# Linear-size squared attention in a hybrid network: look-ahead of the key projections, place of one copy, and place of a yield in the feed-forward

## The chip, the cores and the metric

One Trainium2 chip, one NeuronCore of it. The metric is device time in microseconds from launch to end, all inputs and outputs in HBM, everything in float32. The five engines have queues of their own that run in order: TensorE (PE in the profile, PEld for its weight loads), VectorE (DVE), ScalarE (ACT), GpSimd (POOL) and SyncE (SP), which only issues transfers here. Matmul results go to PSUM, eight banks of 2 KiB per partition.

## The reference

The network has two layers. The first is a 7x7 pairwise self-attention convolution on four images of 256 x 56 x 56; the change doesn't touch it. The second works on the 3136 pixels of each image as tokens of 256 channels: normalise, attend with squared scores, normalise, route half of the tokens through a feed-forward.

```python
qkv = x @ qkv_w.T + qkv_b                      # 8 heads of 32
scores = jnp.einsum('bnhd,bmhd->bhnm', q, k) * scale
t = jnp.square(scores + 5.0)
attn = t / jnp.sum(t, axis=-1, keepdims=True)
out = jnp.einsum('bhnm,bmhd->bnhd', attn, v).reshape(B, N, D)
return out @ proj_w.T + proj_b
...
weights = (jnp.einsum('bsd,do->bso', x, wr) + br)[..., 0]
_, idx = jax.lax.top_k(weights, k)             # k = 1568, of which 1567 are used
h = jax.nn.gelu(jnp.einsum('bkd,dh->bkh', sel, w1) + b1)
y = (jnp.einsum('bkh,hd->bkd', h, w2) + b2) * w_sel[..., None]
processed = jnp.zeros_like(x).at[batch_idx, sel_idx].set(y)
return processed + x
```

## The kernel before

The square of a score is a polynomial of second degree in the key, so no score is ever formed. For each image and each group of four heads a **key stage** runs over 25 tiles of 128 tokens and sums products of key features with the values; the result is a small matrix of coefficients. A **query stage** per image then makes the same features of the queries and multiplies them with the coefficients.

The order of the work is the order in which the program text issues it: each engine keeps that order (`InOrder`), and a tile framework puts semaphores where one instruction needs another or a buffer. Side jobs are generators in a list `later`. `aside()` (line 1678) moves each of them on by one step, and `run(steps)` calls it once after every step of the main work. `run_fast` (line 1844), used in the feed-forward, calls it twice.

A key stage is `keys(b, g)`, line 1198. Three functions make up a tile m:
- `tokens(m)` (line 1203) projects the tokens into keys and values: eight TensorE matmuls into `pv`. One PSUM tile of two banks, `held["kv"]`, takes two tiles of tokens, the even one in the first bank and the odd one in the second; there are two such PSUM tiles (pool `mm`, `bufs=2`). ScalarE copies the keys into `ls` (five buffers) and the values into `v`.
- `features(m)` (line 1223) makes the products of keys with keys, `phi` (two buffers): the squares on ScalarE, eleven of the fifteen remaining distances on VectorE, which reads the keys from PSUM, the others on GpSimd.
- `add(m, phi)` (line 1241) adds values times features into two PSUM banks: `accs` takes the products `phi`; `accq` takes the last distance, the linear sums and, from column P on, the second moments of the keys.

The loop at line 1265 calls `tokens` for the first three tiles, and then at each step `features(m)`, `add(m - 1)`, `tokens(m + 3)` and a `yield`, at which the side jobs run. The first step of image b + 1 is issued inside the query stage of image b.

`coefficients(b, g)`, line 1278, is a side job. Its first step reads `accs` and `accq` in several VectorE instructions and makes `st`; its second makes `line` from column P of `accq`, its third `second` from the next 32 columns (line 1322). `accs` and `accq` lie in a pool of two buffers (`accp`), so the next stage's first `add` needs them free. Further side jobs during a first group (g = 0) are the division, output projection and normalisation of the image before: `divide`, `tokens_out` (po, tk, st, uw in the profile); during a second group the projection of the first queries.

The **feed-forward** takes the 6268 chosen tokens in 13 parts of up to 512. `turn` transposes a part, `first` multiplies by the first weights (ph) with the GELU on ScalarE, `second` (line 1805) by the second weights: for each half of a part 32 matmul instructions (py), then VectorE adds the bias (fz), scales and adds (fy), and GpSimd scatters the rows to the output. While the first parts run, the selection of the last image, `select(b)` (line 1581), is still a side job: eight rounds in which VectorE compares and counts (good, digit, bits, base, tried, hit, per), and TensorE adds the counts over the partitions (pn); then the places (pm, pae, pbe, pas, pbs) and 28 scatters of rows by GpSimd. Parts from number 9 on contain rows of that image; SyncE fetches them after those scatters.

Of the kernel before, what the change touches and what calls it, by code (L numbers as in the profile page):

```python
# [7 lines left out]
F32 = mybir.dt.float32  # L8
I32 = mybir.dt.int32
AF = mybir.ActivationFunctionType  # L10
ALU = mybir.AluOpType
# [4 lines left out]
P = 128  # L16
# [13 lines left out]
DH = 32  # L30
# [6 lines left out]
NT = (HW + P - 1) // P  # L37
# [984 lines left out]
def attn_ffn_layers(  # L1022
# [40 lines left out]
    cp = inner.enter_context(tc.tile_pool(name="coef", bufs=2))  # L1063
    stp = inner.enter_context(tc.tile_pool(name="sums", bufs=1))
    qp = inner.enter_context(tc.tile_pool(name="q", bufs=2))
    ve, te, se, sy, gp = (
        InOrder(tc, e) for e in (nc.vector, nc.tensor, nc.scalar, nc.sync, nc.gpsimd)
    )
# [9 lines left out]
    for i, tag in enumerate(("t", "t", "tr")):  # L1078
        both = tp.tile([P, 2, CH], F32, tag=tag, name=f"rs0_{i}")
        f = slice((2 * i + 1) * CH, (2 * i + 3) * CH)  # L1080
# [10 lines left out]
    kb = const.tile([P, 2, 2 * DH], F32, name="kb")  # L1091
# [102 lines left out]
    def further(a, n):  # L1194

        return bass.AP(a.tensor, a.offset, [*a.ap[:-1], [1, n], a.ap[-1]])

    def keys(b, g):

        vs, ks = {}, {}  # L1200
        size = lambda m: min(P, HW - m * P)

        def tokens(m):

            mn = size(m)
            if m % 2 == 0:
                held["kv"] = mm.tile([P, 2, 512], F32, tag="mm", name=f"pv_{b}_{g}_{m}")
            p = held["kv"][:mn, m % 2]
            for c in range(2):
                matmul(  # L1210
                    p[:, : 2 * P], xn[:, c, m * P : m * P + mn],
                    wqkv[:, c, C:].rearrange("p (i o) -> p i o", i=2)[:, :, g * P : (g + 1) * P],
                    start=c == 0, stop=c == 1,
                )
            k = ks[m] = p[:, :P].rearrange("p (h e) -> p h e", e=DH)
            se.activation(
                lss[m % NKV][:mn, :, LK:LS].rearrange("p h (i e) -> p h i e", i=2),
                k.unsqueeze(2).to_broadcast([mn, 4, 2, DH]), AF.Identity,
            )
            v = vs[m] = kp.tile([P, P], F32, tag="v", name=f"v_{b}_{g}_{m}", bufs=5)  # L1220
            se.activation(v[:mn], p[:, P : 2 * P], AF.Identity)

        def features(m):

            mn = size(m)
            ls, k = lss[m % NKV], ks.pop(m)
            phi = php.tile([P, 4, NF], F32, tag="phi", name=f"phi_{b}_{g}_{m}")
            mine = ls[:mn, :, LK : LK + DH]
            se.activation(phi[:mn, :, :DH], mine, AF.Square)
            at = phi[:mn, :, DH:].rearrange("p h (l e) -> p h l e", e=DH)  # L1230
            for e, of, a, z in ((ve, k, 0, FAR), (gp, mine, FAR, HALF - 1)):
                e.tensor_tensor(
                    at[:, :, a:z], of.unsqueeze(2).to_broadcast([mn, 4, z - a, DH]),
                    further(ls[:mn, :, LK + 1 + a : LK + 1 + a + DH], z - a), ALU.mult,
                )
            gp.tensor_tensor(
                ls[:mn, :, :HALF], mine[:, :, :HALF], mine[:, :, HALF:], ALU.mult
            )
            return phi

        def add(m, phi):
            mn = size(m)
            v, ls = vs.pop(m), lss[m % NKV]
            first, last = m == 0, m == NT - 1
            if first:
                held["sums", b, g] = [
                    accp.tile([P, 512], F32, tag="acc", name=f"acc{i}_{b}_{g}") for i in "sq"
                ]
            accs, accq = held["sums", b, g]
            for h, r in enumerate(QUARTERS):  # L1250
                te.matmul(accs[r], v[:mn, r], phi[:mn, h], start=first, stop=last)
            for h, r in enumerate(QUARTERS):
                te.matmul(
                    accq[r, : LK + DH], v[:mn, r], ls[:mn, h, : LK + DH], start=first, stop=last,
                    skip_group_check=True,
                )

            for h, r in enumerate(QUARTERS):
                k = ls[:mn, h, HALF : LK + DH]
                te.matmul(  # L1260
                    accq[r, P : P + 1 + DH], k[:, 1:], k, start=False, stop=last,
                    skip_group_check=True,
                )

        for m in range(3):
            tokens(m)
        waiting = None
        for m in range(NT):
            phi = features(m)
            if waiting:  # L1270
                add(*waiting)
            waiting = m, phi
            if m + 3 < NT:
                tokens(m + 3)
            yield
        add(*waiting)

    def coefficients(b, g):

        at = f"{b}_{g}"  # L1280
        accs, accq = held.pop(("sums", b, g))
# [2 lines left out]
        ve.tensor_copy(v1, accq[:, HALF:LK])  # L1284
        lin = stp.tile([P, 2 * DH], F32, tag="lin", name=f"lin_{at}")
        linear = accq[:, LK : LK + DH]
        ve.scalar_tensor_tensor(
            lin.rearrange("p (i e) -> p i e", i=2), kb[:, g].rearrange("p (i e) -> p i e", i=2), v1,
            linear.unsqueeze(1).to_broadcast([P, 2, DH]), ALU.mult, ALU.add,
# [15 lines left out]
        ve.tensor_copy(st[:, NF + DH :], lin[:, :DH])  # L1305
        yield

        line = cp.tile([P, 3], F32, tag="line", name=f"line_{at}")
        ve.tensor_copy(line[:, 0:1], accq[:, P : P + 1])
        ve.tensor_scalar(line[:, 1:2], col(f"k_{g}"), float(HW), None, ALU.mult)  # L1310
        ve.tensor_tensor(line[:, 1:2], line[:, 1:2], line[:, 0:1], ALU.add)
        ve.tensor_scalar(line[:, 2:3], line[:, 1:2], 2 * CSHIFT, None, ALU.mult)
# [6 lines left out]
        )  # L1319
        second = stp.tile([P, DH], F32, tag="second", name=f"second_{at}")  # L1320
        ve.scalar_tensor_tensor(
            second, kb[:, g, :DH], line[:, 0:1], accq[:, P + 1 : P + 1 + DH], ALU.mult, ALU.add
        )
        ve.scalar_tensor_tensor(
            second, p[:, :DH], col(f"k_{g}"), second, ALU.mult, ALU.add
        )
        gram = cp.tile([P, P], F32, tag="gram", name=f"gram_{at}")
# [78 lines left out]
    def queries(b):  # L1406
# [54 lines left out]
        if b + 1 < NB:  # L1461
            held["keys"] = keys(b + 1, 0)
            next(held["keys"])
# [286 lines left out]
    for b in range(NB):  # L1750
        held["keys only"] = True
        for g in range(2):
            if g and b + 1 < NB:
                held["t", b + 1, 0] = load(b + 1, 0, "t")
            run(keys(b, g) if b == 0 or g else held.pop("keys"))
            later.append(coefficients(b, g))
            aside()
            if g == 0:
                later.append(project(b, 0))
        later.extend(whole)  # L1760
        whole.clear()
        held["keys only"] = False
        run(queries(b))
# [41 lines left out]
    def second(i):  # L1805

        rows, h = held.pop(("part", i)), held.pop(("h", i))
        y = fp.tile([P, 4, C], F32, tag="y", name=f"fy_{i}")
        for j, (_, pn) in enumerate(parts[i]):

            ve.tensor_scalar(
                y[:pn, j], rows[:pn, j, :C], rows[:pn, j, C + 3 : C + 4],
                rows[:pn, j, C + 2 : C + 3], ALU.mult, ALU.add,
            )
        for m in range(0, len(parts[i]), 2):
            p = accp.tile([P, 2, C], F32, tag="acc", name=f"py_{i}_{m}")
            z = fp.tile([P, 2, C], F32, tag="z", name=f"fz_{i}_{m}")
            both = parts[i][m : m + 2]
            for j, (_, pn) in enumerate(both):
                f = slice((m + j) * P, (m + j) * P + pn)  # L1820
                for e in range(FF // P):
                    te.matmul(
                        p[:pn, j], h[:, e, f], w2[:, e], start=e == 0 and j == 0,
                        stop=e == FF // P - 1, skip_group_check=True,
                    )
            pn, n = both[-1][1], len(both)
            ve.tensor_tensor(
                z[:pn, :n], p[:pn, :n], b2[:pn].to_broadcast([pn, n, C]), ALU.add
            )
            for j, (_, pn) in enumerate(both):  # L1830
                ve.scalar_tensor_tensor(
                    y[:pn, m + j], z[:pn, j], rows[:pn, m + j, C : C + 1], y[:pn, m + j],
                    ALU.mult, ALU.add,
                )
                gp.indirect_dma_start(
                    out.rearrange("b n c -> (b n) c"),
                    bass.IndirectOffsetOnAxis(
                        ap=rows.bitcast(I32)[:pn, m + j, C + 1 : C + 2], axis=0
                    ),
                    y[:pn, m + j], None,  # L1840
                )
            yield

    def run_fast(steps):
        for _ in steps:
# [195 lines left out]
```

## Time and profile before

Three runs took 3243.72, 3245.78 and 3254.06 us, median 3245.78. The profiled execution took 3248.73 us, with a span of 3247.0 us between its first and last instruction and a mean granted TensorE clock of 0.988.

| stretch | us from the span's start |
|---|---|
| convolution layer | 0 to 1442 |
| key stages of image 0, first and second group | 1442 to 1504, 1504 to 1566 |
| query stage of image 0 | 1566 to 1777 |
| key stages of image 1 | 1777 to 1848.5, 1848.5 to 1911 |
| key stages of image 2 | 2133 to 2207.5, 2207.5 to 2270 |
| key stages of image 3 | 2492 to 2565, 2565 to 2628 |
| query stage of image 3 | 2628 to 2845 |
| feed-forward | 2845 to 3247 |

| instruction group | count | mean ns |
|---|---|---|
| TensorE pv, 128x256 | 3136 | 386 |
| VectorE phi, 128x1408 | 200 | 1618 |
| GpSimd phi, 128x512 | 200 | 1241 |
| ScalarE ls, 128x256 | 200 | 387 |

In lines of the profile, `out<-in` names tiles with buffer numbers left out, sizes are partitions x elements, `xN` counts instructions, and a bracket at the end gives idle time of the engine ahead of the line and what ended it. Matmuls overlap, so a TensorE line's duration is longer than its share of the time; distances between starts say more. A line of the timeline begins with start and duration. Nearly all instructions carry one line number, 1007, that of the helper which keeps the order, so groups are told apart by tile names.

### The profile page before, as it was taken

The page shows a single profiled execution, that of the slowest core. Times are in us where ns is not written, and L with a number is a line of the kernel's source. Part 1 is how long each engine was busy: PE and PEld are TensorE (multiplying, and loading weights), DVE is VectorE, ACT ScalarE, POOL GpSimd, SP SyncE. Part 2 cuts the span into 40 slices and gives each one's busy share as a digit, 9 for nine tenths or more (in the row PEclk, how much of TensorE's full clock was granted, in tenths as well). Part 3 has the DMA queues.
Part 4 walks back from the last instruction along what each step waited for, and adds up shares of the span by engine and source line. Part 5 has one row for each costly group of instructions (what it writes and reads, how often), then busy time and mean ns, then how long its engine had stood idle before and what let it go on. Part 6 is the DMA issues. An engine that isn't in the chain of part 4 may idle for free. (4 is left out here: it accounts for less than half of the span.)

```text
span 3247.0 us, 108290 instructions
## 1 busy us (share of the span) xinstructions
PE 3002.4 (92%) x47224; PEld 1311.2 (40%) x47224; DVE 2226.9 (69%) x3019; ACT 1576.1 (49%) x2947; POOL 1726.2 (53%) x1223
## 2 busy tenths in 40 slices
PE   5999999999999999988999799988899899988998
PEld 2333333333333333334333343334333433355666
DVE  4888889898888889888555866568656765443111
ACT  4556556665666665533455344543455345521111
POOL 2898898899989989976200530246022521201311
PEclk9999999999999999999999999999999999998999
DMA  8656676566665756430022102310133001311110
GB/s 233 170 150 176 159 184 183 131 185 179 173 164 155 191 142 163 116 129 19 22 71 57 39 6 65 95 46 20 39 83 82 14 14 48 115 54 35 57 51 23
DMA packets 276497, 327.54 MB, mean 101 GB/s; under 512 B 95985, under 2 KB 269461, under 8 KB 275893
## 3 DMA queue, kind: packets, MB, share of 16 engines
q1 hardware_dynamic: 266037, 298.84, 34.9%
q0 software_dynamic: 7824, 19.48, 1.8%
q8 instruction: 371, 6.08, 0.8%
q10 hardware_dynamic: 2160, 2.29, 0.2%
q14 instruction: 105, 0.86, 0.1%
HBM read 251.51 MB, written 68.51 MB: 99 GB/s over the span
## 5 line engine op out<-in xcount | busy, mean ns | idle before, releaser
L1007 ACT ACTIVATE ph<-pg,unit 128x896 f32<-128x896 f32 x448 | 427.0, 1004 | 402.2 <-PE pg L1007 384.5
L1007 PE MATMUL acc<-pr,same 128*32 128x448 f32 x5376 | 596.7, 545 | 17.9 <-POOL pr L1007 12.0
L1007 POOL TENSOR_TENSOR phi<-ls 128x512 f32<-128x512 f32 (+1 forms) x200 | 248.2, 1241 | 455.7 <-issue 226.3
L1007 POOL TENSOR_TENSOR pr<-xw,w 128x1792 f32<-128x1792 f32 (+2 forms) x126 | 413.6, 3307 | 109.6 <-ACT exp L1007 84.3
L1007 DVE TENSOR_TENSOR pr<-xc,exp 128x1792 f32<-128x1792 f32 (+2 forms) x247 | 441.6, 1839 | 34.4 <-ACT exp L1007 29.9
L1007 DVE TENSOR_TENSOR pr<-xw,exp 128x1792 f32<-128x1792 f32 (+1 forms) x252 | 447.5, 1804 | 2.4 <-DMA xw<-x3d 1.4
L1007 POOL TENSOR_TENSOR pr<-xc,w 128x1792 f32<-128x1792 f32 (+1 forms) x135 | 419.8, 3120 | 12.6 <-ACT w L1007 7.1
L1007 POOL DMA_INDIRECT us<-rows,to x112 | 113.3, 1011 | 576.9 <-DVE rows L1007 334.6
L1007 DVE TENSOR_TENSOR phi<-pv,ls 128x1408 f32<-128x1408 f32 (+1 forms) x200 | 320.8, 1618 | 42.3 <-PE accs L1007 34.5
L1007 PE MATMUL quad<-y,cw 32*32 32x224 f32 (+1 forms) x10752 | 299.3, 456 | 35.1 <-ACT w L1007 19.0
L1007 PE MATMUL pg<-qT,pairs 32*128 32x448 f32 x1792 | 277.2, 588 | 5.7 <-ACT ph L1007 5.3
L1007 PE MATMUL pv<-early,xn 128*32 128x256 f32 x3136 | 213.9, 386 | 58.0 <-DVE phi L1007 40.2
L1007 ACT ACTIVATE ls<-pv 128x256 f32<-128x256 f32 (+1 forms) x200 | 77.4, 387 | 340.0 <-PE pv L1007 317.5
L1007 PEld LDWEIGHTS acc<-pr,same 128*32 128x32 f32 x5376 | 132.6, 109 | 243.4 <-issue 145.8
L1007 PE MATMUL accs<-phi,v 128*32 128x512 f32 (+1 forms) x1600 | 214.8, 599 | 13.7 <-DVE phi L1007 12.3
L1007 PE MATMUL acc<-ph,cf 128*32 128x448 f32 (+1 forms) x1792 | 214.8, 551 | 0.0
L1007 ACT ACTIVATE h<-ph,apar 128x512 f32<-128x512 f32 (+1 forms) x104 | 63.3, 659 | 308.8 <-PE ph L1007 308.8
L1007 ACT ACTIVATE y<-quad,bn2t,bn2s 128x896 f32<-128x896 f32 x112 | 164.5, 1468 | 65.3 <-PE quad L1007 65.3
L1007 DVE TENSOR_REDUCE mm<-quad 128x56 f32<-128x1792 f32 x112 | 172.5, 1540 | 32.3 <-PE quad L1007 31.3
L1007 POOL TENSOR_TENSOR y<-a,ac 128x672 f32<-128x672 f32 x112 | 171.1, 1528 | 36.1 <-DMA ac<-a12d 36.1
L1007 ACT ACTIVATE w<-quad,par 128x1792 f32<-128x1792 f32 x112 | 154.3, 1378 | 69.8 <-PE quad L1007 69.1
L1007 PEld LDWEIGHTS quad<-y,cw 32*32 32x32 f32 x10752 | 85.5, 103 | 249.3 <-issue 119.2
(284 smaller groups left out, 4925.7 us busy)
## 6 DMA issues: line engine op xcount, KB each, us to landing
xw<-x3d SPq DMA_DIRECT2D x54, 992.0 KB
xc<-x3d SPq DMA_DIRECT2D x58, 248.0 KB
xc<-x3d SPq DMA_DIRECT2D x58, 247.5 KB
xc<-x3d SPq DMA_DIRECT2D x58, 247.0 KB
xc<-x3d SPq DMA_DIRECT2D x58, 246.5 KB
x3d<-sx SPq DMA_DIRECT2D x28, 496.0 KB
xr<-in_x_own SPq DMA_DIRECT2D x56, 224.0 KB
xs<-xr SPq DMA_DIRECT2D x224, 56.0 KB
```

What stands on the lines that cost most here:

```text
L1007: return lambda *a, **k: self.tc.keep_in_program_order(of(*a, **k))
```

## The change

There are three edits. The key projections run two tiles ahead of the products instead of three. The second moments (column P and the 32 after it) are copied out of `accq` into a new tile `moments` early in the first step of `coefficients`, and later steps read the copy; `line` is allocated earlier. In `second` the `yield` moves from the end of the loop's body to between the matmuls and VectorE's read of their result, so that the side jobs of that step are issued ahead of fz, fy and the output scatters. There are eight new VectorE instructions in all, one per key stage.

```diff
-        for m in range(3):
+        for m in range(2):
             tokens(m)
         waiting = None
         for m in range(NT):
...
             if waiting:
                 add(*waiting)
             waiting = m, phi
-            if m + 3 < NT:
-                tokens(m + 3)
+            if m + 2 < NT:
+                tokens(m + 2)
             yield
         add(*waiting)
...
         linear = accq[:, LK : LK + DH]
+        line = cp.tile([P, 3], F32, tag="line", name=f"line_{at}")
+        moments = stp.tile([P, 1 + DH], F32, tag="moments", name=f"moments_{at}")
+        ve.tensor_copy(moments, accq[:, P : P + 1 + DH])
...
-        line = cp.tile([P, 3], F32, tag="line", name=f"line_{at}")
-        ve.tensor_copy(line[:, 0:1], accq[:, P : P + 1])
+        ve.tensor_copy(line[:, 0:1], moments[:, 0:1])
...
-            second, kb[:, g, :DH], line[:, 0:1], accq[:, P + 1 : P + 1 + DH], ALU.mult, ALU.add
+            second, kb[:, g, :DH], line[:, 0:1], moments[:, 1:], ALU.mult, ALU.add
...
                         p[:pn, j], h[:, e, f], w2[:, e], start=e == 0 and j == 0,
                         stop=e == FF // P - 1, skip_group_check=True,
                     )
+            yield
             pn, n = both[-1][1], len(both)
             ve.tensor_tensor(
                 z[:pn, :n], p[:pn, :n], b2[:pn].to_broadcast([pn, n, C]), ALU.add
             )
...
                     y[:pn, m + j], None,
                 )
-            yield
```

## The prediction

> **What bounds the kernel now.** I read the page first: TensorE is busy 92% of the span, and the granted clock is full nearly everywhere. The change touches two stretches only: the eight key stages (four images, two groups of heads, 25 tiles each) and the feed-forward at the end. So I went to what TensorE waits for in each.
>
> ```profile
> PE 3002.4 (92%) x47224; PEld 1311.2 (40%) x47224; DVE 2226.9 (69%) x3019; ACT 1576.1 (49%) x2947; POOL 1726.2 (53%) x1223
> ```
>
> The table of TensorE's waits over the stretch with the key stages (1442 to 2628; columns: sum, times, longest):
>
> ```profile
> PE pv L1007 <- DVE phi L1007: 40.2, 37, 3.9
> PE accs L1007 <- DVE phi L1007: 12.3, 29, 0.9
> PE accq L1007 <- DVE second L1007: 9.6, 4, 2.4
> ```
>
> These are the waits the change aims at: a projection (pv) held until VectorE's products (phi) leave the PSUM tile that is reused, and four sums (accq) held by the late read of the second moments. Together 49.8 us, 1.5% of the span. The same stretch in order of time, in a stage with no side work:
>
> ```profile
> 1536.62 1.07 PE L1007 MATMUL pv<-early,xn 128*32 128x256 f32 x16
> 1537.50 1.04 PE L1007 MATMUL accs<-phi,v 128*32 128x512 f32 x8
> 1538.51 1.05 PE L1007 MATMUL pv<-early,xn 128*32 128x256 f32 x16
> 1538.78 1.62 DVE L1007 TENSOR_TENSOR phi<-pv,ls 128x1408 f32<-128x1408 f32 x1 [0.35 <-PE accs L1007]
> 1539.69 0.39 ACT L1007 ACTIVATE ls<-pv 128x256 f32<-128x256 f32 x1 [1.12 <-PE pv L1007]
> 1539.97 0.27 ACT L1007 ACTIVATE v<-pv 128x128 f32<-128x128 f32 x1
> 1540.46 0.85 PE L1007 MATMUL pv<-early,xn 128*32 128x256 f32 x12
> ```
>
> Two tiles take 1540.46 - 1536.62 = 3.84 us, with TensorE idle under 0.1 of it. So in steady state there is almost nothing to win; the waits sit where VectorE has side work. Now the opening of the stage of image 1, where two tiles share one PSUM tile just as everywhere:
>
> ```profile
> 1778.15 0.27 ACT L1007 ACTIVATE v<-pv 128x128 f32<-128x128 f32 x1
> ...
> 1778.47 1.93 PE L1007 MATMUL pv<-early,xn 128*32 128x256 f32 x32 [0.67 <-ACT v L1007]
> ...
> 1779.89 0.27 ACT L1007 ACTIVATE v<-pv 128x128 f32<-128x128 f32 x1
> 1780.25 1.62 DVE L1007 TENSOR_TENSOR phi<-pv,ls 128x1408 f32<-128x1408 f32 x1 [2.40 <-ACT v L1007]
> ```
>
> The products of tile 0 need only tile 0, whose copies ended at 1778.42. They start at 1780.25, when ScalarE has copied tile 1 out of the other half. So the products of an even tile wait for projection and copies of the odd tile beside it: 1780.25 - 1778.47 = 1.78 us after that projection starts. Today that is paid once per stage, because projections run three tiles ahead.
>
> Feed-forward, TensorE alone:
>
> ```profile
> 2900.18 7.07 PE L1007 MATMUL py<-xn,h 128*128 128x256 f32 x32
> 2911.15 0.25 PE L1007 MATMUL pn<-per,aones 112*32 112x15 f32 x8 [3.90 <-DVE per L1007]
> 2911.33 8.86 PE L1007 MATMUL py<-xn,h 128*128 128x256 f32 x32
> 2924.11 0.30 PE L1007 MATMUL pn<-per,aones 112*32 112x15 f32 x8 [3.92 <-DVE per L1007]
> 2924.34 6.12 PE L1007 MATMUL ph<-fu,xn 128*128 128x512 f32 x8
> ```
>
> The counting matmul pn of the last image's selection stands behind a batch of py, and its input (per) stands on VectorE behind fz and fy, which wait for that batch. TensorE idles 3.9 us, and the next batch runs slowly: 8.86 for what took 7.07. The windows name the cause; the third number from the end is the granted clock:
>
> ```profile
> 2900.00:2907.30 7.30, 7.25 (x36) 6.07 (x33) 2.53 (x6) 1.91 (x4) 0.00 (x0) 1.00 0.00 0
> 2911.30:2920.20 8.90, 8.89 (x40) 7.18 (x33) 0.00 (x0) 0.00 (x0) 0.96 (x1) 0.81 0.22 66
> 2924.30:2930.40 6.10, 6.10 (x18) 2.39 (x11) 2.02 (x7) 0.00 (x0) 0.96 (x1) 0.59 0.35 99
> ```
>
> Granted clock 1.00 before the wait, 0.81 and 0.59 after.
>
> **Keys two ahead.** No instruction is added. Projection of tile m+2 now follows the sums of tile m-1. It reuses a tile read by products m-1 at the latest, which those sums needed anyway: the 40.2 us wait goes. In exchange the odd neighbour m+1 is projected just before the sums of m-1, and the even products m wait for its copies. With S the start of the even sums: next projection S + 1.01 (1537.50 to 1538.51), neighbour copied and products start 1.78 later, the sums that wait for them start 1.77 after that (1560.22 to 1561.99 in this trace). Pair: 1.01 + 1.78 + 1.77 = 4.56 against 3.84, +0.72. TensorE's own work is 2 x (1.01 + 0.87) = 3.76, so it idles 0.8 per pair. What is queued behind the late products on VectorE is the odd tile's products, 1.53 later and in time, and the side jobs; behind the waiting sums on TensorE is the next projection.
>
> I then walked each kind of stage tile by tile: an instruction starts when its engine is done with the one ahead and what it waits for has ended, with these spacings and with the side jobs at the durations of their rows. The walk of the old order gives 62.2, 71.1 and 58.5 us, the trace 62.5 (1503.90 to 1566.4), 71.7 (1776.76 to 1848.5) and 61.9 (1442.0 to 1503.9).
> - Second group, four stages: the sums of tile 6 come 3.8 us earlier (24.2 into the stage, not 28.0), since the 2.39 us hold of accq and the pv waits in the coefficients' side work are gone. From there to tile 22 seven pairs lose 0.72 each and the eighth, which had no projection ahead of its sums, 1.5: 6.6. The last tiles return 0.4: 64.7 against 62.2, +2.4 each, +9.6.
> - First group of images 1 to 3: side work of VectorE (statistics 1.6, uw 1.9, scaling 2.0, waits for po) reaches to tile 16. There the old projections waited 9.9 to 11.2 us; tile 16 comes 4.1 earlier (51.5, not 55.6), three clean pairs lose 2.6, the end returns 0.4: 69.2 against 71.1, -1.9 each, -5.7.
> - First stage: one scaling of 1.0 each third tile, which falls into VectorE's new slack; ten pairs lose 0.7 each: +6 (walk +6.6).
> Sum +10. The price of a pair is what the trace of before cannot show in steady state. 51 pairs carry it (32, 9 and 10); at half of 0.72 the sum is 18 lower, at one and a half times 18 higher: bounds -8 and +28. I take the full 0.72, since each of its three parts is a row.
>
> The wait for the neighbour is one place to weigh a rule. The Trainium skill, PSUM — Partial Sum Buffer, section on bank collisions, asks for guards by bank and quadrant. Tile 0 and tile 1 lie in different banks, so by it the products need not wait for the neighbour; the row above (2.40 us) shows that here they do. What the bank rule would make of the time is the first rival.
>
> **Moments copied first.** Eight copies of 128x33 from PSUM, not in the trace: between 0.14 (copy of 128x1) and 0.28 (lin, 128x64), taken as 0.19. Four lie ahead of the first products of a second group (in the walk), four at the start of the queries, where VectorE idles 1.42 before them; uncovered they cost 0.8 in all. Alone the edit frees little: the projection behind accq waited for the same products, ended 1513.83, and ran at 1514.27. It pays only together with the shorter look-ahead.
>
> **Feed-forward.** No instruction is added; TensorE's order stays. On VectorE the selection's chain (good to per, 2908.81 to 2911.01, 2.2 us) moves ahead of fz and fy, so it runs under the 7.07 us of py. Removed: 3.90 + 3.92 + 3.92 (2950) + 2.96 (pm, 2964) = 14.7. After a second half, fz and fy come between: py end to pn is then 3.9, and a ph batch of 3.70 plus 0.18 covers it; nothing new. With the waits goes the slow running: 8.86 - 7.07, 6.12 - 3.70, 10.03 - 7.07, 5.10 - 3.70 = 8.6. Sum -23.3, bounds -13 and -24. On POOL two row scatters now go ahead of two output scatters (2.85 us apart, so 5.7 later); the rows of part 9, which SP fetches behind them until 3105, are used at 3140.7. SP's order stays. The tail from 3000 on is TensorE without gaps, so the gain reaches the end.
>
> The second place: the Trainium skill, TensorE: Matmul & The Clock Gate, Part 1, says half rate follows an idle window of about 3.4 us and lasts about as long. By it three waits are long enough and cost 1.7 each, an estimate of 5.1 instead of 8.6 and 3236 for the sum; the rows also show 5.10 for 3.70 after a wait of 2.96, so the rows stand.
>
> **Sum.** 3248.73 (profiled execution, span 3247.0) + 10 - 23.3 = 3235.4. It lay 3.0 above the median of the runs, 3245.78, so 3232 there.
>
> **Rivals.**
> 1. The products wait by bank only. Then no pair is slower: the same walk gives 57.9, 64.9 and 56.4, so 4 x -4.3, 3 x -6.2, -2.1 = -38; with -23.3: 3185. For it: no data of the neighbour is used. Against it: the 2.40 us row.
> 2. Slower: the neighbour's copies set the pace in all stages, with no early gains, because side work sits in VectorE's program order between even and odd products and delays both. 12 pairs x 0.72 x 8 = +69, less 23.3: +46, 3291; it decides from where the stages lose over 2.9 us each (23.3 / 8). For it: VectorE is busy 56 of 73 us in image 1. Against it: its waits on the sums, up to 0.7 a tile, shrink with the old pv wait.
> 3. No change: the clock also stays low behind the 1.8 us wait for per_sign (2891.8), which is not touched, and only the waits go: +10 - 14.7, 3241.
>
> **Chances.** Forecast 0.68 (own range 3219 to 3243), rival 1 0.06, rival 2 0.14, rival 3 0.12. 0.3% is 9.7 us, about what a measurement can tell from none. Faster: 0.56 of the forecast plus rival 1, 0.62; same: 0.12 + 0.12 + 0.01, 0.25; slower 0.13. Range: -8 - 24 gives 3214, +28 - 13 gives 3261, of which I leave out the top, where both bounds would have to meet: 3214 to 3257.
>
> **What would show it.** Right: products of even tiles waiting for ACT v in all stages, pairs of 4.5 to 4.6 us, no accq wait for second, pv waits gone; no pn wait over 0.5 after 2890 and py at 7.07. Wrong: pairs of 3.8 (rival 1), or first-group stages longer than 74 us (rival 2), or a granted clock under 0.9 after 2900 (rival 3).

## The result, and the profile after

The changed kernel takes 3223.69 us (median of six, 3218.65 to 3233.17), the kernel before 3245.38 (six, 3243.39 to 3254.06). The ratio is 0.993, 95% interval 0.9908 to 0.9951: faster by 16 to 30 us. The forecast was 3232, in a range of 3214 to 3257.

The profiled execution of the changed kernel is the longest of its six, 3233.17 us with a span of 3231.4. Cut at the same marks as the kernel before (a key stage ends with the copy of `v1` out of accq, which the trace prints as v<-accq; the feed-forward starts with the first ft), the two spans compare as follows:

| stretch, us | before | changed | difference |
|---|---|---|---|
| convolution, to the first pv | 1442.0 | 1451.1 | +9.1 |
| first stage, image 0 | 62.1 | 69.1 | +7.0 |
| first groups of images 1, 2, 3 | 71.9, 74.8, 73.7 | 69.2, 69.3, 69.9 | -2.6, -5.6, -3.9 |
| second groups of images 0 to 3 | 62.4, 62.7, 62.4, 62.4 | 64.5, 64.5, 64.5, 63.7 | +2.1, +1.8, +2.1, +1.3 |
| query stages, sum | 870.3 | 871.0 | +0.7 |
| feed-forward, to the end | 402.3 | 374.7 | -27.6 |

The key stages together lose 2.3 us. The feed-forward makes the whole gain. The convolution, whose code is the same, varies: it ended between 1432.1 and 1451.1 us in the nine profiled executions of this study. Its +9.1 here lies within that range. This execution lies 9.5 above its kernel's median; how much of that is the convolution can't be said, since each kernel has one trace.

The page of the changed kernel:

```profile
PE 2998.0 (93%) x47224; PEld 1309.7 (41%) x47224; DVE 2217.6 (69%) x3027; ACT 1574.0 (49%) x2947; POOL 1724.8 (53%) x1223
```

VectorE has eight instructions more (3027 against 3019), the copies of the moments; nothing else is new. TensorE's waits over the key stages (sum, times, longest):

```profile
PE accs L1007 <- DVE phi L1007: 28.1, 42, 7.8
PE accs L1007 <- POOL phi L1007: 18.1, 32, 0.8
PE accs L1007 <- ACT v L1007: 15.8, 26, 0.6
```

No projection waits for products any more (40.2 us before), and accq no longer waits for second (9.6). In their place the sums accs wait, 62 us in these three rows where 12.3 stood. Together TensorE's waits inside the eight stages come to 84.8 us, against 80.4 before: they moved and did not leave. What VectorE waits for tells why, first before and then changed:

```profile
DVE phi L1007 <- ACT v L1007: 7.5, 4, 2.4
DVE phi L1007 <- ACT v L1007: 85.9, 63, 3.2
```

Before, it came four times, all in the first groups of images 1 to 3, and not once in every stage as the prediction says. Now it comes 63 times, in all eight stages, for 96 even tiles that have an odd neighbour (12 in each stage). One steady pair in order of time:

```profile
1555.98 0.38 PE L1007 MATMUL pv<-early,xn 128*32 128x256 f32 x1
...
1558.65 0.38 PE L1007 MATMUL pv<-early,xn 128*32 128x256 f32 x1
...
1560.07 0.27 ACT L1007 ACTIVATE v<-pv 128x128 f32<-128x128 f32 x1
...
1560.42 3.15 DVE L1007 TENSOR_TENSOR phi<-pv,ls 128x1408 f32<-128x1408 f32 x2 [1.39 <-ACT v L1007]
...
1560.53 0.38 PE L1007 MATMUL pv<-early,xn 128*32 128x256 f32 x1
```

The projection of the odd neighbour starts at 1558.65, ScalarE has copied it at 1560.34, and only then VectorE makes both tiles' products. The pair takes 1560.53 - 1555.98 = 4.55 us. The feed-forward, TensorE alone:

```profile
2905.60 0.23 PE L1007 MATMUL pnsign<-per_sign,aones 112*32 112x1 f32 x8 [1.81 <-DVE per_sign L1007]
2905.76 3.70 PE L1007 MATMUL ph<-fu,xn 128*128 128x512 f32 x8
...
2910.50 7.07 PE L1007 MATMUL py<-xn,h 128*128 128x256 f32 x32
2917.50 0.25 PE L1007 MATMUL pn<-per,aones 112*32 112x15 f32 x8
2917.68 7.17 PE L1007 MATMUL py<-xn,h 128*128 128x256 f32 x32
```

No bracket at pn, and the second py of the part takes 7.17 us where it took 8.86. From 2849.8 to 3225.3 us the granted clock is 1.00 throughout. The first two lines hold something that the forecast left as it was: behind the wait for per_sign, which is as long as before, ph takes 3.70 us and not 5.40. In the kernel before:

```profile
2893.58 0.23 PE L1007 MATMUL pnsign<-per_sign,aones 112*32 112x1 f32 x8 [1.82 <-DVE per_sign L1007]
2893.75 5.40 PE L1007 MATMUL ph<-fu,xn 128*128 128x512 f32 x8
```

### The profile page after: what moved, and what is told of

It is laid out like the page before. It is cut to its first block, busy times and chain, and to the rows that moved or that the text cites. A ratio compares the mean times of both kernels' runs of the same rounds, so it can differ in the third digit from the quotient of the medians.

```text
span 3231.4 us, 108046 instructions
## 1 busy us (share of the span) xinstructions
PE 2998.0 (93%) x47224; PEld 1309.7 (41%) x47224; DVE 2217.6 (69%) x3027; ACT 1574.0 (49%) x2947; POOL 1724.8 (53%) x1223
## 5 line engine op out<-in xcount | busy, mean ns | idle before, releaser
L1007 DVE TENSOR_TENSOR phi<-pv,ls 128x1408 f32<-128x1408 f32 (+1 forms) x200 | 317.3, 1616 | 87.7 <-ACT v L1007 85.9
L1007 PE MATMUL accs<-phi,v 128*32 128x512 f32 (+1 forms) x1600 | 214.5, 602 | 74.9 <-DVE phi L1007 28.1
L1007 ACT ACTIVATE y<-quad,bn2t,bn2s 128x896 f32<-128x896 f32 x112 | 164.4, 1468 | 66.3 <-PE quad L1007 66.2
L1007 PEld LDWEIGHTS quad<-y,cw 32*32 32x32 f32 x10752 | 85.9, 103 | 249.8 <-issue 123.7
```

The source lines that it names most:

```text
L1007: return lambda *a, **k: self.tc.keep_in_program_order(of(*a, **k))
```

## The experiments

All seven were timed beside the kernel before; a ratio is to that kernel, with its 95% interval. The stages of their profiled executions stand in one table; a first group is given for images 1, 2 and 3, a second for images 0 to 3.

| us | first stage | first groups | second groups | key stages, sum | feed-forward |
|---|---|---|---|---|---|
| before | 62.1 | 71.9, 74.8, 73.7 | 62.4, 62.7, 62.4, 62.4 | 532.3 | 402.3 |
| changed | 69.1 | 69.2, 69.3, 69.9 | 64.5, 64.5, 64.5, 63.7 | 534.6 | 374.7 |
| yield only | 61.9 | 72.9, 75.2, 73.8 | 62.4, 64.3, 62.4, 62.4 | 535.3 | 375.1 |
| keys and moments | 68.8 | 69.3, 69.2, 69.6 | 64.5, 64.5, 64.5, 63.7 | 534.1 | 401.4 |
| keys only | 68.8 | 69.3, 69.3, 69.3 | 69.4, 68.6, 68.5, 65.7 | 548.8 | 401.8 |
| moments only | 62.2 | 75.2, 73.5, 74.9 | 62.1, 62.1, 62.4, 62.1 | 534.5 | 397.9 |
| one bank, two ahead | 61.0 | 65.7, 65.7, 65.7 | 59.0, 57.6, 57.6, 56.4 | 488.6 | 374.5 |
| one bank, three ahead | 59.1 | 66.2, 66.2, 66.5 | 57.3, 57.3, 57.3, 56.1 | 486.0 | 374.4 |
| one bank, three ahead, no moments | 61.0 | 66.2, 66.6, 66.5 | 61.0, 61.2, 61.4, 58.5 | 502.3 | 376.6 |

**The yield alone.** To the kernel before:

```diff
                         stop=e == FF // P - 1, skip_group_check=True,
                     )
+            yield
...
                     y[:pn, m + j], None,
                 )
-            yield
```

> The kernel before with the yield of the feed-forward's second layer moved, and nothing else. Theory (the gain is made in the feed-forward alone): the waits of pn and pm (14.7 us) and the slow running behind them go, the stretch from the first ft to the end is 375 us as in the changed kernel (before: 402.3), key stages as before (62 us for a second group, 71 to 75 for a first group of images 1 to 3): 24 to 28 us faster than before, 3218 to 3222, which is the changed kernel's time or a little less. Rival (the shorter look-ahead earns its own part): clearly slower than the changed kernel, 3230 or more. Side question: the ph batch behind the 1.8 us wait for per_sign, 5.40 us before and 3.70 in the changed kernel, shows which of the two it is here; the wait is the same in all three.

Measured: 3218.76 us, ratio 0.9917 (0.9894 to 0.994). Its feed-forward takes 375.1 us, its key stages 535.3. That is the changed kernel's gain; the two intervals overlap, so no difference between this and the whole change is shown. On the side question: the wait for per_sign is 1.82 us here, and ph behind it takes 3.70, as in the changed kernel.

**Keys and moments, without the yield.** The two key edits of the change applied to the kernel before.

> The changed kernel with the yield put back: keys two ahead and the copy of the moments alone. Theory: the eight key stages together within 2 us of the changed kernel's, which are 2.3 us longer than before by the stages of the two profiled executions (first stage +7.0, second groups +1.3 to +2.2, first groups of images 1 to 3 -2.6 to -5.6); the feed-forward takes 402 again: 3245 to 3255, no change to 0.3% slower than before. Rival (look-ahead earns): 3240 or less. Rival (the prediction's second, all stages pay): over 3265.

Measured: 3244.07 us, ratio 1.000 (0.9981 to 1.0018), 1 us under the range expected. The key part as a whole earns nothing and costs nothing that can be measured; the feed-forward is back at 401.4, with pn waits of 3.91, 3.92 and 3.93 us and a py of 10.11 behind the first.

**Keys alone.**

```diff
-        for m in range(3):
+        for m in range(2):
             tokens(m)
...
-            if m + 3 < NT:
-                tokens(m + 3)
+            if m + 2 < NT:
+                tokens(m + 2)
```

> The kernel before with the keys projected two tiles ahead, and nothing else: no copy of the moments, the yield at its old place. Theory: without the copy the sums accq of a second group wait for the line and second of the coefficients as before (about 2.4 us each), and with one projection less in hand this is not made up: a second group takes 67 us by the tile walk, 2.3 more than with the copy, so 4 x 2.3 = 9 us slower than the run with keys and moments: 3254 to 3264. Rival (the copy pays nothing in either order): as keys and moments, within 3 us.

Measured: 3264.43 us, ratio 1.0043 (1.0025 to 1.0061), slower, and 20 us slower than with the copy of the moments, run on the same chip; 9 were expected. TensorE at the opening of the second group of image 0, and the window behind it (the granted clock is the third number from the end):

```profile
1519.81 0.39 PE L1007 MATMUL accq<-ls,v 128*32 128x49 f32 x8 [2.53 <-DVE second L1007]
...
1520.08 1.94 PE L1007 MATMUL pv<-early,xn 128*32 128x256 f32 x16
```

```profile
1518.10:1524.90 6.80, 5.09 (x59) 2.21 (x62) 2.11 (x4) 0.75 (x3) 1.23 (x2) 0.50 0.01 2
```

The wait itself is 2.5, as said. What was left out is the clock: from 1518.1, still within the wait, it is at half for 6.8 us, and sixteen instructions of a projection take 1.94 where they take 1.07 otherwise. This group took 69.4, the walk had said 67. The four second groups separate the wait from the clock: accq waits 2.53 in each, and the first three have slow stretches with it (6.8, 3.4 and 3.4 us at 0.50) and take 68.5 to 69.4, while the fourth has none and takes 65.7, 2.0 more than with the copy. By the stages the missing copy costs 548.8 - 534.1 = 14.7; where the rest of the 20 lies was not traced, and the convolution's spread is larger than it.

**Moments alone.**

```diff
+        moments = stp.tile([P, 1 + DH], F32, tag="moments", name=f"moments_{at}")
+        ve.tensor_copy(moments, accq[:, P : P + 1 + DH])
...
-        ve.tensor_copy(line[:, 0:1], accq[:, P : P + 1])
+        ve.tensor_copy(line[:, 0:1], moments[:, 0:1])
...
-            second, kb[:, g, :DH], line[:, 0:1], accq[:, P + 1 : P + 1 + DH], ALU.mult, ALU.add
+            second, kb[:, g, :DH], line[:, 0:1], moments[:, 1:], ALU.mult, ALU.add
```

> The kernel before with the copy of the moments alone: keys three ahead, the yield at its old place. Theory: the accq wait goes (9.6 us in four stages), but the projection queued behind accq waits for the products anyway, so the wait moves to pv: 62.1 to 62.4 us for a second group, no change within 3 us, 3243 to 3248. Rival (the copy alone gives its wait back): 9 us faster, 3236.

Measured: 3246.36 us, ratio 0.9992 (0.9976 to 1.0008), no change. TensorE at the same place:

```profile
1512.87 0.27 PE L1007 MATMUL accq<-ls,v 128*32 128x49 f32 x8
1512.95 0.24 PE L1007 MATMUL accq<-ls 128*32 128x33 f32 x8
1515.29 1.07 PE L1007 MATMUL pv<-early,xn 128*32 128x256 f32 x16 [2.09 <-DVE phi L1007]
```

In the kernel before, accq stood here with 2.39 us idle and the pv behind it with none. Now accq has no wait and pv waits 2.09 for products. The sums over the stages say the same: accq 9.6 to nothing, pv for products 40.2 to 48.3.

**One bank for each tile, two ahead.** To the changed kernel. The four banks are a pool of four single tiles while keys run, and the pool of two wide ones otherwise:

```diff
+    def four_banks(halves):
+        nonlocal mm, kv
+        wide.close()
+        kv = mm = None
+        if halves:
+            kv = wide.enter_context(tc.tile_pool(name="attn_kv", bufs=4, space=PSUM))
+        else:
+            mm = wide.enter_context(tc.tile_pool(name="attn_mm", bufs=2, space=PSUM))
+
+    four_banks(True)
...
-            if m % 2 == 0:
-                held["kv"] = mm.tile([P, 2, 512], F32, tag="mm", name=f"pv_{b}_{g}_{m}")
-            p = held["kv"][:mn, m % 2]
+            p = kv.tile([P, 512], F32, tag="kv", name=f"pv_{b}_{g}_{m}")[:mn]
...
+            four_banks(True)
             held["keys"] = keys(b + 1, 0)
...
+        four_banks(False)
         run(queries(b))
```

> The changed kernel with a PSUM tile of one bank for each tile of tokens (four of them, in the four banks that the two wide ones had), so that an even tile and its odd neighbour share none. Nothing is computed otherwise. Theory (the products of even tiles wait for the neighbour because both lie in one PSUM tile): the waits of the products for ACT v go, a pair of tiles takes 3.8 us instead of 4.55, and by the tile walk a second group takes 57.9 us (64.3 in the changed kernel), a first group of images 1 to 3 64.0 (69.4), the first stage 56.4 (69.1): 4 x 6.4 + 3 x 5.4 + 12.7 = 54 us faster than the changed kernel, 3165 to 3180. Rival (what holds the products is the one ScalarE queue or VectorE's side work, the neighbour only ended last): the stages lose under 15 us together, 3209 or more.

Measured: 3172.05 us, ratio 0.9789 (0.9772 to 0.9806); against the changed kernel that is 0.9789 / 0.993 = 0.986, or 46 us. The key stages fall from 534.6 to 488.6, also 46, and VectorE's wait for the neighbour is:

```profile
DVE phi L1007 <- ACT v L1007: 2.2, 3, 0.7
```

85.9 us in 63 times became 2.2 in 3. The second groups took 56.4 to 59.0 (57.9 expected). The 8 us short of 54 lie in the first stage, 61.0 where the walk gave 56.4, and in the first groups, 65.7 for 64.0 three times.

**One bank for each tile, three ahead.** To the kernel of the run just told, `range(3)` and `m + 3` in the loop.

> As the run with one bank and two ahead, but with the keys three tiles ahead as in the kernel before. Theory: with four single banks the third projection ahead costs nothing (tile m + 3 takes the bank of tile m - 1, whose products the sums ahead of it needed anyway): 57.5, 64.6 and 56.0 us by the walk, within 4 us of the run with two ahead; the length of the look-ahead did not matter by itself, only which tiles share a PSUM tile. Rival (two ahead is better by itself, as the change has it): 10 us or more slower than with two ahead.

Measured: 3168.09 us, ratio 0.9766 (0.975 to 0.9782), the lowest median of the study and 2.3% below the kernel before; its interval overlaps that of the run with two ahead, so the two can't be told apart. Its key stages sum to 486.0, 2.6 from those with two ahead. Steady state:

```profile
1535.00 1.62 DVE L1007 TENSOR_TENSOR phi<-pv,ls 128x1408 f32<-128x1408 f32 x1 [0.25 <-PE accs L1007]
...
1535.58 1.07 PE L1007 MATMUL accs<-phi,v 128*32 128x512 f32 x8
...
1539.32 1.07 PE L1007 MATMUL accs<-phi,v 128*32 128x512 f32 x8
```

The two lines of accs are two tiles apart: 1539.32 - 1535.58 = 3.74 us, and VectorE now waits for TensorE. So neither two nor three is the right look-ahead by itself: what counted was which tiles share a PSUM tile.

**One bank, three ahead, without the moments.** The lines of the copy taken out of the kernel of the run just told.

> As the run with one bank and three ahead, without the copy of the moments: line and second read accq as in the kernel before. Theory: the accq wait comes back (about 2.4 us in each second group) and no projection behind it hides it now: second groups 59.9 us instead of 57.5, 4 x 2.4 = 10 us slower than with the copy. Rival (as in the kernel before, the copy pays nothing with three ahead): within 3 us.

Measured: 3187.07 us, ratio 0.9829 (0.9813 to 0.9845): 19.0 slower than with the copy, run on the same chip, where 10 were expected. By the stages it is 502.3 - 486.0 = 16.3, and of the other 2.2 in the profiled executions, in the feed-forward, 1.7 is a slow stretch behind the wait for per_sign, which has nothing to do with the copy. So the copy that is worth nothing in the kernel before is worth some 16 here. The accq wait, and the projection behind it:

```profile
1513.36 0.39 PE L1007 MATMUL accq<-ls,v 128*32 128x49 f32 x8 [2.53 <-DVE second L1007]
...
1513.62 1.95 PE L1007 MATMUL pv<-early,xn 128*32 128x256 f32 x16
```

Again the wait is the expected 2.5 and a stretch at half clock comes on top (granted 0.50 from 1512.7 to 1516.1). The first three second groups, each with such a stretch, lose 3.7 to 4.1; the fourth has the same wait and no slow stretch, and loses the 2.4 that were expected.

## Why the prediction came out as it did

**Keys two ahead.** Expected +10 with bounds -8 and +28; the profiled stages give +2.3, and the run of the key part alone 1.000. The mechanism held in every sign that was promised: products wait for ACT v in all stages, pairs of 4.55 (4.56 said), no pv wait for products, no accq wait. The walk's lengths for the new order also held for two kinds of stage: 64.7 against 63.7 to 64.5 for a second group, 69.2 against 69.2 to 69.9 for a first group of images 1 to 3. The first stage was put at 58.5 in the old order and 65.1 in the new and took 62.1 and 69.1, so the walk is some 4 short in both; its difference is right because the two errors cancel. What was mis-sized is the old length of the first groups. All three were put at the 71.1 of image 1's walk, while the trace of before had 74.8 and 73.7 for images 2 and 3. So the saving was -2.6, -5.6 and -3.9 instead of 3 x -1.9, and that is most of the 8 us between +10 and +2.3.

**The neighbour.** The one bank runs show that the shared PSUM tile is the cause: apart from the tiles and their pools nothing was changed, and the wait left. The Trainium skill, PSUM — Partial Sum Buffer, section on bank collisions, asks for guards where accesses meet in one bank and quadrant. The wait here was wider than that, by PSUM tile over two banks, and the rival that took the rule at its word (3185) failed for the changed kernel for this reason. With one tile to a bank the wait went, and the second groups and first groups shrank to nearly what the rival's walk had given, 57.6 and 65.7 against 57.9 and 64.9; the first stage took 61.0 against 56.4.

**Moments.** Said to free little alone and to pay only with the shorter look-ahead. Alone: no change, and the wait moved to pv as argued. With the shorter look-ahead it pays 15 us by the stages and 20 by the medians, where the walk has 9; the clock is what the walk lacks, as the fourth second group shows, which has the wait without the slow stretch.

**Feed-forward.** -23.3 was expected, with -24 as the far bound; it came to -27.6. The removed waits (14.7) and the slow batches behind them (8.6) are all gone. The rest is two more slow batches: ph behind per_sign, 5.40 to 3.70, and ph behind a late fu, 15.70 to 14.00, together 3.4. Their waits, 1.8 and 1.96 us, are the same before and after. The prediction has TensorE without gaps from 3000 on; the wait for fu at 3141.7 and the slow stretch behind it were there and were left out. The third rival had the batch behind per_sign slow for good; in the changed kernel it is not, and the last section shows what goes with that. The last 1 us lies at the end: from the start of the last py it took 13.1 us before and takes 12.0 now.

The last two amounts are luck of the two executions that were compared, not the work of the moved yield. With the yield at its old place ph takes 3.70 behind per_sign in the keys and moments run, and 14.00 behind fu in the moments only run; with the new place it takes 5.40 behind per_sign in the run with one bank and three ahead without the moments. The end takes 12.0 in the keys and moments run too. Over the nine executions the feed-forward takes 397.9 to 402.3 us with the old place, 400.9 in the mean, and 374.4 to 376.6 with the new, 375.1 in the mean: the yield is worth some 26 of the 27.6, still more than the far bound of 24 that the prediction gave it.

**The slower rival.** It decided from 2.9 us lost per stage. No second group lost over 2.1, and first groups of images 1 to 3 gained. Only the first stage behaved as it said, with 7.0.

**The sum.** 3248.73 - 13.3 was the forecast for a profiled execution, which took 3233.17 with a convolution 9.1 longer; the rest moved by -24.7. At the median the gain is 21.7 where 13.3 was forecast: 4 more from the feed-forward, 8 more from the keys by the trace, less what the convolution's spread of some 19 us blurs.

## What to carry to other kernels

A look-ahead is counted in buffers, but it waits in units of what the scheduler tracks: before changing its depth, check whether two of its steps share one tile, and split that tile first. A wait that is worth nothing to remove can hide behind another that is due at the same moment, and become worth its full length when that one goes, so an edit without effect deserves a second run after the next one. A short wait of TensorE can cost more than its length in clock, so price it with the batch behind it.

## What the runs showed of the hardware

Slow stretches of TensorE's clock begin on a grid. The moments at which the granted clock drops, read from windows of 1 us (the share of the window at 0.50 gives the moment to some 0.1 us), were in the kernel before 2895.12, 2912.18, 2922.42, 2953.14, 2966.80 and 3144.28. From the first they lie 17.06, 27.30, 58.02, 71.68 and 249.16 us away: 5, 8, 17, 21 and 73 times 3.413. In the moments only run, four later drops lie 5, 9, 17 and 21 times 3.41 from its first. The grid lies elsewhere in each execution. In all nine traces the slow stretches, 138 in number, begin on such a grid with a step of 3.4133 us, within 1 ns. Call the time from one of its points to the next a cell. What a wait of 1.8 us costs goes with where it falls. In the kernel before, the wait for per_sign (2891.76 to 2893.58) lies inside one cell; this cell and the next:

```profile
2891.70:2895.10 3.40, 1.58 (x12) 0.86 (x12) 2.67 (x9) 1.75 (x3) 0.00 (x0) 1.00 0.00 0
2895.10:2898.50 3.40, 3.40 (x5) 1.35 (x4) 0.00 (x0) 0.00 (x0) 0.00 (x0) 0.50 0.00 0
```

The first figure behind the length is TensorE's busy time: 1.58 of 3.40 us, under half, and the next cell runs at 0.50, which costs 1.7. In the changed kernel the grid is known from a drop at 2846.40; by it a cell ends at 2904.4, within the same wait (2903.79 to 2905.60):

```profile
2901.00:2904.40 3.40, 2.79 (x7) 0.95 (x5) 3.33 (x6) 2.46 (x4) 0.00 (x0) 1.00 0.58 173
2904.40:2907.80 3.40, 2.20 (x13) 1.24 (x14) 1.99 (x9) 1.18 (x3) 0.00 (x0) 1.00 0.01 3
```

Both cells are over half busy, and no slow one follows. Each of the nine executions has this wait and the one for fu, 1.96 us. Of these 18, seven lay inside one cell and had a slow cell behind them, and ten were split by a border and had none. One doesn't fit: in the keys and moments run the wait for per_sign starts with its cell, TensorE is busy 1.65 of its 3.40 us, and the next cell is at full clock. A cell of the moments only run is like it: it is busy 1.55, holds the start of a longer wait, and the next one is at full clock. Counted over all cells of the nine traces that start after 1460 us at full clock, with busy times from the exact points of the grid: of 52 with TensorE busy under 1.4 us every one has a slow cell behind it, of 24 with 1.4 to 1.6 us twelve have one, and of 4472 with more a single one. So the border lies between 1.4 and 1.6 of 3.41 us in these traces; what decides inside it is open, and no kernel was made to place a wait on the grid.

The Trainium skill, TensorE: Matmul & The Clock Gate, Part 1, calls the window free-running and 3413 ns long, which the grid agrees with. It names an idle window as what brings the drop; here waits of 1.82 and 1.96 us, some half of a window, were enough where they lay inside one cell.
